# Which quads' C products GpSimdE takes in a Mamba scan, and in which order

## The chip, the cores and the metric

The kernel runs on one core of a Trainium2 chip. The time is the device time of one execution in microseconds (us), the median of some runs. Engines: TensorE (PE in the profile) does matmuls, VectorE (DVE) scans and elementwise work, ScalarE (ACT) activations, GpSimdE (POOL) elementwise work on SBUF only, SyncE (SP) issues the transfers.

## The reference

The input x is (2, 256, 64, 64) in fp32: two batches of 4,096 tokens with 256 channels. Layer 0 is a group norm, a Mamba block with 256 inner channels and a residual. Layer 1 is a layer norm, then a Mamba block forward and one backward (512 inner channels each), residuals, and a mixture of eight small MLPs on all tokens. One Mamba block, cut to what matters here:

```
xs, z = x @ W_in
xs = silu(causal_conv4(xs)); dbc = xs @ W_x
dt = softplus(dbc[:16] @ W_dt + b); B, C = dbc[16:32], dbc[32:48]      # 16 states
h[t, d, s] = exp(dt[t, d] * A[d, s]) * h[t-1, d, s] + dt[t, d] * xs[t, d] * B[t, s]
y[t, d] = sum_s h[t, d, s] * C[t, s] + xs * D
out = (y * silu(z)) @ W_out
```

## The kernel before

The tokens lie along the free axis in chunks of 512, the channels on the 128 partitions. A *job* is one Mamba pass of one batch (layer 0 twice, forward twice, backward twice), a *step* is one chunk of a job: 48 steps, the first 16 narrow (256 inner channels: two blocks of 128, one pair), then 16 forward and 16 backward ones, wide (four blocks, two pairs). For each pair of blocks the 16 states are taken two at a time: a *quad* is two states by two blocks, 128 x 2,048 numbers, n = 0 to 7 counts the quads of a pair, g counts all 640. So a narrow step has one group of eight quads and a wide step two: here called half A (first pair) and half B (second pair).

A quad goes through these functions:

- `load_bc` (line 488) brings the B and C rows of two states from DRAM, broadcast to all partitions (tiles `bc0` and `bc1`, four buffers each).
- `emit_b` (511): GpSimdE makes the product of `xdt` (dt times xc, made at line 509 once per eight quads) and B into the tile `bq` (six buffers). This is the *B product*.
- `emit_decay` (524): ScalarE makes the decays `da` in PSUM, two tiles of two states' halves in turn.
- `emit_scan` (535): VectorE runs four scans of 512 tokens, one per state and block. For even n the result goes into `bq`, for odd n into `da`.
- The *C product*: for even n `emit_times_c_quad` (560) on GpSimdE, in place on `bq`, after `emit_carry` (555), where ScalarE saves the last column as the next chunk's start; for odd n `emit_times_c` (546) on VectorE, with a small copy (549) of the last column.
- `emit_sum` (569): TensorE adds the four parts of `bq` to `y` in PSUM with an identity matrix. The `bq` buffer is free once its sum is done.
- `emit_gate` (585): VectorE multiplies `y` with the gate `sz`; `emit_skip` (578) begins the next `y`, of which there is one buffer.

Beside this the next step's projections are made (`prepare`): in_proj (`xs`, 326) with a copy by ScalarE (351), the convolution as four diagonal matmuls (361), two activations `thx` (370, 371) and VectorE's `xc` (375), x_proj (387), softplus in three activations `sp` (417 to 419) and VectorE's `dt` (423), the gate's `z` and `sz` (444). They share two PSUM buffers (`psp`). `finish` does the output projection (600) and the residual (608) of the step before. `norm` makes the layer norms of the next step. The functions are put into numbered slots for a queue (`Slots`), two slots to a quad, and `prepare` staggers PE, ACT and DVE work by one slot each.

The emission loop at the end runs through the quads and, for both states of each, emits a slot's work for each engine. Every engine's queue is in order. But the framework's scheduler orders the instructions of each queue by priority and by its own estimate of readiness, and assigns tile buffers as they come free in it, so a queue need not stand in the order in which the source emits it.

In the loop GpSimdE's part was, at the first state of each odd n:

```
emit_times_c_quad(g - 1)
want_b(g + 2, g + 3)
want(1, g + 1, g + 2)
want(0, g + 4, g + 5)
```

`want_b` emits B products whose rows are loaded, `want` queues loads (0 for B, 1 for C rows) in one list that `flush` empties from its head. The last stage, the MLPs, comes after all scans.

Of the kernel before, what the change touches and what calls it, by code (L numbers as in the profile page):

```python
# [32 lines left out]
ALU = mybir.AluOpType  # L33
# [7 lines left out]
NS = 16  # L41
DTR = 16
QN = NS // 2
E = 8
V_CW, V_CB, V_DB, V_D, V_A = 0, 4, 5, 6, 7
NV = V_A + NS
# [37 lines left out]
def hybrid_kernel(ctx: ExitStack, tc: tile.TileContext, a: dict, out: bass.AP):  # L84
    nc = tc.nc
# [46 lines left out]
    with ExitStack() as st:  # L132
# [98 lines left out]
        steps = [(job, c) for job in jobs for c in range(NCH)]  # L231
        cks = [{} for _ in steps]
        tags = [f"{n}_{c}" for n in range(len(jobs)) for c in range(NCH)]

        def norm(i, s0, sl):

            (job, c), ck, tag = steps[i], cks[i], tags[i]
            s = job.cols(c)
            b = job.batch

            def alloc():
                ck["nx"] = wk.tile([P, KC, T], F32, tag="nx", name=f"nx_{tag}", bufs=2)

            if job.flip:
                def load():
                    alloc()
                    nc.sync.dma_start(ck["nx"], n2_dram[b][:, NCH - 1 - c, :, :])
                sl.put(s0, "sp", load)
                return

            def load_x():
                alloc()
                ck["x"] = wk.tile([P, KC, T], F32, tag="x", name=f"x_{tag}")
                src = t_dram[b] if job.layer else a["x"][b].rearrange("(k p) l -> p k l", p=P)
                nc.sync.dma_start(ck["x"], src[:, :, s])

            sl.put(max(s0 - 4, 0), "sp", load_x)
            if job.layer == 0:
                def scale():
                    for k in range(KC):  # L260
                        nc.scalar.activation(
                            ck["nx"][:, k, :], ck["x"][:, k, :], AF.Identity,
                            bias=job.gb[:, k : k + 1], scale=job.gs[:, k : k + 1],
                        )
                sl.put(s0, "act", scale)
                return

            def mean():  # L270
                ck["ps"] = psp.tile([P, T], F32, tag="ps", name=f"mean_{tag}")
                for k in range(KC):
                    nc.tensor.matmul(
                        ck["ps"], mean_w, ck["x"][:, k, :], start=(k == 0), stop=(k == KC - 1)
                    )

            def centre():
                ck["cen"] = wk.tile([P, KC, T], F32, tag="cen", name=f"cen_{tag}")
                nc.vector.tensor_tensor(ck["cen"], ck["x"], over_channels(ck["ps"]), ALU.subtract)

            def square():
                ck["n1"] = wk.tile([P, KC, T], F32, tag="n1", name=f"n1_{tag}")
                nc.scalar.activation(ck["n1"], ck["cen"], AF.Square)

            def variance():
                ck["var"] = psp.tile([P, T], F32, tag="ps", name=f"var_{tag}")
                for k in range(KC):
                    nc.tensor.matmul(
                        ck["var"], mean_w, ck["n1"][:, k, :], start=(k == 0), stop=(k == KC - 1)
                    )  # L290

            def roots():
                ck["r1"] = psp.tile([P, T], F32, tag="ps", name=f"r1_{tag}")
                rsqrt(ck["r1"], ck["var"], eps5)
                rsqrt(ck["var"], ck["var"], eps10, scale=1.0 + 1e-5)

            def divide():
                nc.vector.tensor_tensor(ck["n1"], ck["cen"], over_channels(ck["r1"]), ALU.mult)
                nc.vector.tensor_tensor(ck["cen"], ck["cen"], over_channels(ck["var"]), ALU.mult)

            def add():
                nc.gpsimd.tensor_tensor(ck["x"], ck["x"], ck["n1"], ALU.add)

            def affine():
                for k in range(KC):
                    nc.scalar.activation(
                        ck["nx"][:, k, :], ck["cen"][:, k, :], AF.Identity,
                        bias=lngb[:, 1, k : k + 1], scale=lngb[:, 0, k : k + 1],
                    )

            def store():
                nc.sync.dma_start(n2_dram[b][:, c, :, :], ck["nx"])
                nc.sync.dma_start(t_dram[b][:, :, s], ck["x"])

            for d, queue, fn in (
                (0, "pe", mean), (1, "dve", centre), (1, "act", square), (2, "pe", variance),
                (3, "act", roots), (4, "dve", divide), (4, "pool", add), (5, "act", affine),
                (6, "sp", store),
            ):
                sl.put(s0 + d, queue, fn)  # L320

# [15 lines left out]
        def prepare(i, s0, sl, rate=1):  # L337
# [115 lines left out]
            if c == 0:  # L453
                if "in" not in w:
                    load_weights(job, tag, sl)
                    s0 = max(s0, 4)
# [12 lines left out]
            s0 += nj // rate  # L469
            if i + 1 < len(steps):  # L470
                norm(i + 1, s0, sl)
                s0 += 5 if steps[i + 1][0].layer and not steps[i + 1][0].flip else 1
            for j in range(nj):
                put(s0 + j, gate(j))
            return s0 + nj + 2
# [4 lines left out]
        ]  # L480
        nq = len(quads)
        bq, bt, ct, da, y = {}, {}, {}, {}, {}
        loads, wanted = [], []

        def load_bc(g, h, store):
            i, _, n = quads[g]
            t = bcp.tile([P, 2, T], F32, tag=f"bc{h}", name=f"bc{h}_{g}")
            nc.sync.dma_start(t, cks[i]["bc"][h, 2 * n : 2 * n + 2, :].partition_broadcast(P))
            store[g] = t

        def want(h, *gs):
            loads.extend((h, g) for g in gs if g < nq)

        def flush():
            while loads and "bc" in cks[quads[loads[0][1]][0]]:
                h, g = loads.pop(0)
                load_bc(g, h, ct if h else bt)

        def want_b(*gs):
            wanted.extend(g for g in gs if g < nq)  # L500
# [25 lines left out]
                    scale=steps[i][0].w["a"][:, 2 * jp + j, 2 * n + s : 2 * n + s + 1],  # L526
                )

        def emit_scan(g, s):
            i, jp, n = quads[g]  # L530
            job, c = steps[i]
            d = da[g, s]
            for j in range(2):
                b = bq[g][:, s, j, :]
                nc.vector.tensor_tensor_scan(  # L535
                    d[:, j, :] if n % 2 else b, d[:, j, :], b,
                    job.h[:, 2 * n + s, 2 * jp + j : 2 * jp + j + 1] if c else 0.0,
                    ALU.mult, ALU.add,
                )

        def emit_times_c(g, s):

# [16 lines left out]
        def emit_times_c_quad(g):  # L559
            nc.gpsimd.tensor_tensor(  # L560
                bq[g], bq[g],
                ct[g].rearrange("p s (o t) -> p s o t", o=1).to_broadcast([P, 2, 2, T]), ALU.mult,
            )

        def emit_sum(g, ss):
            i, jp, n = quads[g]
            for s in ss:
                for j in range(2):
                    nc.tensor.matmul(  # L569
                        y[i, jp][:, j, :], ident, bq[g][:, s, j, :], start=False,  # L570
                        stop=(n == QN - 2 and s == 1),
                    )

        def emit_skip(i, jp):
# [52 lines left out]
        sl = Slots()  # L627
# [4 lines left out]
        sl.drain(end + 8)  # L632
        want(0, 0, 1, 2)
        want(1, 0, 1)
        want(0, 3, 4)
        flush()
        want_b(0, 1, 2)
        emit_decay(0, 0)
# [3 lines left out]
        for i, (job, c) in enumerate(steps):  # L642
# [3 lines left out]
            if i:  # L646
                finish(i - 1, 3 if wide else 5, sl)
            if i + 1 < len(steps):
                prepare(i + 1, 5 if wide else 0, sl, 1 if wide or steps[i + 1][0].nj == 2 else 2)
            if i < 4:  # L650
                def chunk_stats(k, c=c):
                    v = {}
# [23 lines left out]
            for q in range(np_ * QN):  # L676
                g = g0 + q
                _, jp, n = quads[g]
                for s in range(2):
# [5 lines left out]
                    if first == 2 and last is not None:  # L685
                        emit_gate(*last)
                        last = None
                    sl.run(slot, "dve")

                    if first == 3:  # L690
                        emit_skip(i, jp)
                    sl.run(slot, "pe")
                    if s == 0:
                        if n % 2 == 0:
                            if g >= 1:
                                emit_sum(g - 1, (1,))
                            if g >= 2:
                                emit_sum(g - 2, (0, 1))
                                bq.pop(g - 2)
                                bq.pop(g - 1)  # L700
                                ct.pop(g - 2)
                                ct.pop(g - 1)
                    elif n % 2:
                        emit_sum(g, (0,))
                    if first == 0 and g:
                        pi, pjp, _ = quads[g - 1]
                        last = (pi, pjp)

                    if s == 0 and n % 2:
                        emit_carry(g - 1)  # L710
                    if s == 0:
                        emit_decay(g, 1)
# [1 line left out]
                        emit_decay(g + 1, 0)  # L714
                    sl.run(slot, "act")

                    if s == 0 and n % 2:
                        emit_times_c_quad(g - 1)
                        want_b(g + 2, g + 3)
                        want(1, g + 1, g + 2)  # L720
                        want(0, g + 4, g + 5)
                        flush()
                    sl.run(slot, "pool")

                    emit_scan(g, s)
                    if n % 2:
                        emit_times_c(g, s)
            if sl.at:
                sl.drain(64)
                flush()  # L730
                want_b()
                emit_decay(g + 1, 0)
        g = nq - 1
        emit_sum(g, (1,))
        emit_sum(g - 1, (0, 1))
        i = len(steps) - 1
        emit_gate(i, steps[i][0].nj // 2 - 1)
        sl = Slots()
# [211 lines left out]
```

## Time and profile before

| what | value |
|---|---|
| median of 3 runs (lowest, highest) | 7373.88 us (7371.5, 7379.04) |
| the profiled execution, its span | 7371.24 us, 7369.5 us |
| scans of all quads | from 57 us to 5,601 us |
| MLP stage | from 5,620 us to the end |
| busy TensorE, VectorE, ScalarE, GpSimdE | 83%, 63%, 48%, 62% |
| mean granted TensorE clock | 0.909 |

A share of busy time is taken over the whole span, with the MLP stage in it, where GpSimdE has nothing to do. A group row gives: line, engine, operation, output and inputs with their shapes, count, then busy us and mean ns of one, then the idle time of the engine just before these instructions and what ended most of it. A row of waits gives: who waited, for whom, us in total, times, longest. A row of busy time by stretch gives: the stretch in us from the span's start, its length, then for PE, its weight loads, DVE, ACT and POOL the busy us and count, then the TensorE clock, the DMA share and GB/s. A timeline row gives start, length, engine, line, operation, tiles and count, and in brackets the idle time before it.

### The profile page before, as it was taken

Reading aid. Unit: us, or ns where it says so; the run is one execution under the profiler, and the core shown is the slowest. Engines: PE = TensorE matmul, PEld = TensorE weight load, DVE = VectorE, ACT = ScalarE, POOL = GpSimd, SP = SyncE. Lnnn points to the kernel's source line nnn. Section 1 sums busy time; section 2 is a strip of 40 time slices with the busy share of each in tenths; the row PEclk is TensorE's granted clock in tenths of the full one; section 3 lists DMA queues with packets and bytes.
Section 4 is the critical chain, followed back from the end, with each engine's and each line's share of the span. In section 5 each row is a group of like instructions: output and inputs, shape, how many; then the busy total and the mean of one; then the engine's idle time right before and its main releaser. Section 6 shows DMA issues by size and latency. Waiting matters only on the chain.

```text
span 7369.5 us, 43337 instructions
## 1 busy us (share of the span) xinstructions
PE 6102.4 (83%) x13160; PEld 2613.7 (35%) x13160; DVE 4677.5 (63%) x4889; ACT 3559.7 (48%) x5295; POOL 4535.2 (62%) x1062
## 2 busy tenths in 40 slices
PE   6888778878787888877777778777776999999999
PEld 2333333333333333333333333333333444444444
DVE  6889877778877877877787777787784111111111
ACT  7887556455445555544544544544542222222222
POOL 6889878878878878877887887887883000000000
PEclk8999989999999999988989889888887999999999
DMA  5444434434433443443343343343332000000000
GB/s 187 147 155 167 157 132 158 143 132 140 144 128 132 146 138 129 146 143 129 129 143 124 132 140 123 126 145 125 128 132 94 8 4 12 12 12 12 12 1 11
DMA packets 254189, 806.30 MB, mean 109 GB/s; under 512 B 26362, under 2 KB 35330, under 8 KB 253954
## 3 DMA queue, kind: packets, MB, share of 16 engines
q1 hardware_dynamic: 253954, 803.53, 32.6%
q8 instruction: 103, 1.69, 0.1%
q14 instruction: 132, 1.08, 0.0%
HBM read 749.95 MB, written 53.48 MB: 109 GB/s over the span
## 4 chain that ended last, share of the span: by engine, by line
POOL 27%; PE 22%; issue 16%; DVE 2%; ACT 1%; DMA 1%; POOLq 0%; SPq 0%; DVEq 0%; ACTq 0%
POOL bq L511 19%; PE hp L835 13%; POOL bq L560 7%; PE ym L869 6%; PE wb L860 1%; POOL xdt L509 1%; PE lg L805 1%; PE var_m L125 1%; DVE bq L535 1%; DVE da L535 1%; PE ym L855 0%; DMA t_dram<-xr 0%; ACT L108 0%; DVE cen_m L118 0%; DMA xr<-t_dram 0%
## 5 line engine op out<-in xcount | busy, mean ns | idle before, releaser
L511 POOL TENSOR_TENSOR bq<-xdt,bc 128x2048 f32<-128x2048 f32 x640 | 2880.7, 4523 | 555.0 <-PE y L569 553.4
L524 ACT ACTIVATE da<-dt,w_a 128x512 f32<-128x512 f32 x2564 | 1751.9, 689 | 1965.6 <-DVE h_state L549 1010.4
L569 PE MATMUL y<-bq,ident 128*128 128x512 f32 x5120 | 2363.6, 608 | 88.1 <-POOL bq L560 51.2
L535 DVE TENSOR_TENSOR_SCAN bq<-da,h_state,bq 128x512 f32<-128x512 f32 x1120 | 1360.0, 1267 | 631.9 <-POOL bq L511 605.2
L560 POOL TENSOR_TENSOR bq<-bq,bc 128x2048 f32<-128x2048 f32 x320 | 1447.6, 4524 | 311.8 <-ACT h_state L555 305.8
L569 PEld LDWEIGHTS y<-bq,ident 128*128 128x128 f32 x5120 | 1002.4, 197 | 1397.3 <-issue 1262.0
L535 DVE TENSOR_TENSOR_SCAN da<-da,h_state,bq 128x512 f32<-128x512 f32 x1120 | 1410.7, 1280 | 61.2 <-ACT da L524 31.4
L839 ACT ACTIVATE h<-hp,of,sc 128x512 f32<-128x512 f32 x512 | 398.4, 778 | 1024.1 <-PE hp L835 1024.1
L361 PE MATMUL conv<-xs,w_conv 128*128 128x512 f32 x1280 | 681.0, 682 | 249.0 <-ACT xs L351 248.1
L546 DVE TENSOR_TENSOR bq<-da,bc 128x1024 f32<-128x1024 f32 x640 | 778.8, 1218 | 12.7
L578 PE MATMUL y<-xc,w_d 128*128 128x512 f32 x320 | 275.0, 1009 | 541.2 <-DVE sz L585 541.2
L866 DVE TENSOR_TENSOR h<-h,wbs 128x1024 f32<-128x1024 f32 x128 | 156.9, 1226 | 874.7 <-ACT h L839 874.7
L361 PEld LDWEIGHTS conv<-xs,w_conv 128*128 128x128 f32 x1280 | 273.8, 219 | 641.5 <-issue 333.8
L835 PE MATMUL hp<-n,W 128*128 128x512 f32 x1024 | 490.4, 633 | 0.0
L835 PE MATMUL hp<-h,W 128*128 128x512 f32 x1024 | 449.9, 592 | 0.0
L869 PE MATMUL ym<-h,Wo 128*128 128x512 f32 x1024 | 449.9, 592 | 0.0
L326 PE MATMUL z<-nx,w_in 128*128 128x512 f32 x640 | 321.6, 635 | 133.4 <-DVE sz L444 76.7
L578 PEld LDWEIGHTS y<-xc,w_d 128*128 128x128 f32 x320 | 88.7, 303 | 680.5 <-DVE sz L585 599.7
L326 PE MATMUL xs<-nx,w_in 128*128 128x512 f32 x640 | 302.5, 604 | 15.0 <-DVE sz L444 5.9
L600 PE MATMUL o<-sz,w_out 128*128 128x512 f32 x640 | 311.9, 624 | 1.1 <-DVE sz L444 0.8
L835 PEld LDWEIGHTS hp<-n,W 128*128 128x128 f32 x1024 | 200.9, 202 | 293.4 <-issue 293.4
L509 POOL TENSOR_TENSOR xdt<-dt,xc 128x1024 f32<-128x1024 f32 x80 | 188.4, 2355 | 187.8 <-DVE dt L423 165.1
(121 smaller groups left out, 4424.2 us busy)
## 6 DMA issues: line engine op xcount, KB each, us to landing
bc<-bcd SPq DMA_DIRECT2D x1280, 512.0 KB, 3.9
t_dram<-xr SPq DMA_DIRECT2D x48, 512.0 KB, 3.6
x<-t_dram SPq DMA_DIRECT2D x32, 512.0 KB, 5.7
xr<-t_dram SPq DMA_DIRECT2D x32, 512.0 KB, 5.2
x<-in_x SPq DMA_DIRECT2D x16, 512.0 KB, 5.1
xr<-in_x SPq DMA_DIRECT2D x16, 512.0 KB, 3.8
t_dram<-x SPq DMA_DIRECT2D x16, 512.0 KB, 3.1
n_dram<-nx SPq DMA_DIRECT2D x16, 512.0 KB, 4.0
```

The costliest lines, as they stand in the source:

```text
L326: nc.tensor.matmul(ps, job.w["in"][:, k, m * P : (m + 1) * P], rhs, start=(k == 0), stop=(k == KC - 1),)
L361: nc.tensor.matmul(v["ps"], w["conv"][:, j, k, :], job.xs[:, j, k : k + T], start=(k == 0), stop=(k == 3),)
L511: nc.gpsimd.tensor_tensor(bq[g], ck["xdt", jp].rearrange("p (o j) t -> p o j t", o=1).to_broadcast([P, 2, 2, T]), bt.pop(g).rearrange("p s ...
L524: nc.scalar.activation(da[g, s][:, j, :], cks[i]["dt", jp][:, j, :], AF.Exp, scale=steps[i][0].w["a"][:, 2 * jp + j, 2 * n + s : 2 * n + s ...
L535: nc.vector.tensor_tensor_scan(d[:, j, :] if n % 2 else b, d[:, j, :], b, job.h[:, 2 * n + s, 2 * jp + j : 2 * jp + j + 1] if c else 0.0, ...
L546: nc.vector.tensor_tensor(bq[g][:, s, :, :], d, ct[g][:, s : s + 1, :].to_broadcast([P, 2, T]), ALU.mult)
L560: nc.gpsimd.tensor_tensor(bq[g], bq[g], ct[g].rearrange("p s (o t) -> p s o t", o=1).to_broadcast([P, 2, 2, T]), ALU.mult,)
L569: nc.tensor.matmul(y[i, jp][:, j, :], ident, bq[g][:, s, j, :], start=False, stop=(n == QN - 2 and s == 1),)
L578: nc.tensor.matmul(y[i, jp][:, j, :], job.w["d"][:, 2 * jp + j, :], cks[i]["xc", jp][:, j, :], start=True, stop=False,)
L835: nc.tensor.matmul(ps, w[:, k, m * P : (m + 1) * P], x[:, k, :], start=(k == 0), stop=(k == KC - 1),)
L839: nc.scalar.activation(h[:, m, :], ps, AF.Relu, bias=of[:, l, e, m : m + 1], scale=sc[:, l, e, m : m + 1],)
L869: nc.tensor.matmul(y[:, b, m, :], we["Wo", e][:, k, m * P : (m + 1) * P], h2[b][:, k, :], start=False, stop=(e == E - 1 and k == KC - 1),)
```

## The change

GpSimdE takes the C products of quads 0, 2, 3 and 5 of each eight in place of 0, 2, 4 and 6. A table `POOL_C` gives for each of these the later quad at whose start its sum is emitted on TensorE (0 at 2, 2 at 4, 3 at 5, 5 at 7). A table `POOL_AT` gives the order in which GpSimdE's products are emitted at the start of a quad ("c0 b4 b5" at quad 1: the C product of quad 0, then the B products of quads 4 and 5), and each B product emits the load of the B rows three quads later. C rows are wanted two quads ahead, one per quad, and the loads of B and C rows have lists of their own. VectorE's slot work (projections) is emitted between the two scans of a state in place of ahead of them. `prepare` begins one slot earlier in wide steps, and the normalisation's activations and later parts are one slot later. The core of the diff:

```diff
+POOL_C = {0: 2, 2: 4, 3: 5, 5: 7}
+POOL_AT = {0: "b3", 1: "c0 b4 b5", 3: "c2 b6", 4: "c3 b7", 6: "c5 b8 b9", 7: "b10"}
...
-                (0, "pe", mean), (1, "dve", centre), (1, "act", square), (2, "pe", variance),
-                (3, "act", roots), (4, "dve", divide), (4, "pool", add), (5, "act", affine),
-                (6, "sp", store),
+                (0, "pe", mean), (1, "dve", centre), (2, "act", square), (3, "pe", variance),
+                (4, "act", roots), (5, "dve", divide), (6, "pool", add), (6, "act", affine),
+                (7, "sp", store),
...
-        def emit_scan(g, s):
+        def emit_scan(g, s, j):
...
+            b = bq[g][:, s, j, :]
+            nc.vector.tensor_tensor_scan(
+                b if n in POOL_C else d[:, j, :], d[:, j, :], b,
...
-                prepare(i + 1, 5 if wide else 0, sl, 1 if wide or steps[i + 1][0].nj == 2 else 2)
+                prepare(i + 1, 4 if wide else 0, sl, 1 if wide or steps[i + 1][0].nj == 2 else 2)
...
-                    sl.run(slot, "dve")
...
+                        if g and (n - 1) % QN not in POOL_C:
+                            emit_sum(g - 1, (1,))
+                        for m, due in POOL_C.items():
+                            if due == n:
+                                emit_sum(g - n + m, (0, 1))
+                    elif n not in POOL_C:
                         emit_sum(g, (0,))
...
-                    if s == 0 and n % 2:
-                        emit_times_c_quad(g - 1)
-                        want_b(g + 2, g + 3)
-                        want(1, g + 1, g + 2)
-                        want(0, g + 4, g + 5)
+                    if s == 0:
+                        for what in POOL_AT.get(n, "").split():
+                            m = g - n + int(what[1:])
+                            if what[0] == "c":
+                                emit_times_c_quad(m)
+                            else:
+                                want(0, m + 3)
+                                flush()
+                                want_b(m)
+                    else:
+                        want(1, g + 2)
                         flush()
                     sl.run(slot, "pool")
 
-                    emit_scan(g, s)
-                    if n % 2:
+                    emit_scan(g, s, 0)
+                    sl.run(slot, "dve")
+                    emit_scan(g, s, 1)
+                    if n not in POOL_C:
                         emit_times_c(g, s)
```

## The prediction

> **What bounds the kernel now.** Read the page's first part and the three groups of the scan loop, then the waits, then the busy time by half step.
>
> ```profile
> PE 6102.4 (83%) x13160; PEld 2613.7 (35%) x13160; DVE 4677.5 (63%) x4889; ACT 3559.7 (48%) x5295; POOL 4535.2 (62%) x1062
> ...
> L511 POOL TENSOR_TENSOR bq<-xdt,bc 128x2048 f32<-128x2048 f32 x640 | 2880.7, 4523 | 555.0 <-PE y L569 553.4
> ...
> L535 DVE TENSOR_TENSOR_SCAN bq<-da,h_state,bq 128x512 f32<-128x512 f32 x1120 | 1360.0, 1267 | 631.9 <-POOL bq L511 605.2
> L560 POOL TENSOR_TENSOR bq<-bq,bc 128x2048 f32<-128x2048 f32 x320 | 1447.6, 4524 | 311.8 <-ACT h_state L555 305.8
> ```
>
> No engine is full. All GpSimdE work lies in the 5,540 us of the scans: 80 groups of eight quads, each 12 products of 4.52 us and one xdt of 2.36, so 56.6 us per group. The waits show a ring: VectorE waits for GpSimdE's B products, these wait for TensorE's sums to free a buffer, TensorE waits for ScalarE's copies:
>
> ```profile
> DVE bq L535 <- POOL bq L511: 694.3, 243, 7.5
> ...
> POOL bq L511 <- PE y L569: 553.4, 85, 10.1
> POOL bq L560 <- ACT h_state L555: 305.8, 201, 7.7
> ...
> PEld conv L361 <- ACT xs L351: 303.9, 68, 6.5
> ```
>
> Busy time by half step: two halves (A, then B) of a backward step, then of a forward step.
>
> ```profile
> 4087.80:4154.90 67.10, 52.16 (x109) 22.22 (x108) 51.85 (x53) 25.84 (x42) 53.92 (x13) 0.85 0.48 157
> 4154.90:4227.80 72.90, 57.46 (x126) 24.46 (x125) 56.75 (x60) 41.09 (x64) 58.63 (x15) 0.93 0.33 109
> 2681.10:2749.40 68.30, 57.01 (x117) 24.09 (x116) 53.98 (x57) 27.45 (x46) 56.20 (x15) 0.88 0.51 169
> 2749.40:2823.90 74.50, 58.41 (x127) 24.57 (x126) 57.76 (x60) 46.71 (x71) 58.54 (x15) 0.93 0.33 107
> ```
>
> Columns: length, then busy us of PE, its loads, DVE, ACT, POOL. A backward step takes 140.0 us with VectorE busy 108.6: it stands 31.4. So the time is set by who stands ahead of whom in the queues. GpSimdE's timeline shows it:
>
> ```profile
> 4127.71 9.00 POOL L511 TENSOR_TENSOR bq<-xdt,bc 128x2048 f32<-128x2048 f32 x2 [1.81 <-PE y L569]
> 4137.45 4.52 POOL L560 TENSOR_TENSOR bq<-bq,bc 128x2048 f32<-128x2048 f32 x1 [0.73 <-ACT h_state L555]
> 4150.39 8.98 POOL L511 TENSOR_TENSOR bq<-xdt,bc 128x2048 f32<-128x2048 f32 x2 [8.42 <-PE y L569]
> 4160.10 4.52 POOL L560 TENSOR_TENSOR bq<-bq,bc 128x2048 f32<-128x2048 f32 x1 [0.73 <-ACT h_state L555]
> ```
>
> One C product, two B products, one C product: the two Bs wait for a late sum, and no B product is ahead.
>
> **What the skill says.** The Trainium skill, "GPSIMD Engine Reference", Performance versus the Vector engine: a two-input fp32 operation on 2048 elements takes 4497 ns on GpSimdE; here 4523 and 4524. "TensorE: Matmul & The Clock Gate", The HAM clock gate: after an idle window of about 3.4 us the array runs at half rate until busy for as long. Agrees: eight convolution instructions took 6.62 us after 4.03 us of idleness, 3.60 without.
>
> ```profile
> 4138.53 6.62 PE L361 MATMUL conv<-xs,w_conv 128*128 128x512 f32 x8 [4.03 <-ACT xs L351]
> ```
>
> "ScalarE: Activation LUTs", What ACT_TABLE_LOAD costs: 1283 ns and a drain of about 1380. The trace has the 1283; the next activation starts 0.02 us after it, so I charge 1.28.
>
> **The change part by part.** Work on GpSimdE, TensorE and VectorE keeps its count and size: four C products per group, 12 GpSimdE products, the same scans. So nothing is gained or lost in busy time there; only order counts. The built program (its queues can be read without running it) does not hold the order in the table POOL_AT: the scheduler moves products by its own estimate. In the built program of before, a wide group reads c0 b2 b3 c2 b4 b5 c4 b6 b7 c6 b0' b1' (b is a quad's B product, c its C product, ' the next group), as the timeline above has it. After, in backward steps:
>
> - A: c0 b2 b3 b4 c2 b5 c3 c5 b6 b7 b8
> - B: c8 b9 b10 c10 b11 b12 c11 b13 x b14 c13 b15 x b0' b1'
>
> In forward steps A is c0 b3 b4 c2 b5 c3 c5 b6 b7 b8, and B has x c13 b14 b15 x, add, b0' b1' b2'. So c5 stands ahead of b6, c8 of b9, c10 of b11, c11 of b13: the next quad's B product waits behind a C product that can't begin before the scan just done. Behind that B product stand VectorE's scan, then ScalarE's decays (they need the scan's PSUM tile back) with the projection's copies, then TensorE's convolutions and sums.
>
> I work this as a timetable with the durations of before's trace: a product 4.52; a quad whose C is on GpSimdE 4.8 (four scans, 4.81 in VectorE's timeline); a quad with C on VectorE 7.4 (4137.00 to 4144.47); from scan to C product 0.4 (ScalarE's carry copy); two matmuls of a sum 1.72. t is 0 at the first scan of A in a backward step.
>
> A. c0 5.2 to 9.7, b2 to 14.3, b3 18.8, b4 23.3, c2 27.8, b5 32.3, c3 36.8. VectorE: q1 to 12.2, q2 14.3 to 19.1, q3 to 23.9, q4 with the gate and one residual add to 33.2, q5 with the other to 38.7. c5 (carry at 38.3) to 42.9, b6 47.4, b7 51.9: q6 starts at 47.5, **8.8 idle**. TensorE gets the gate at 26.3, does skip, output projection, sums 5 and 0, and the first convolution by 48.9, the third xs by 50.6; its copy on ScalarE stands behind the decays of q7, which wait for q6 (54.9), so it ends at 58.5. The second convolution runs cold, 58.6 to 65.2, then sum 2 to 68. b8 needs that buffer: 68 to 72.6. q7 ended at 63.5: **9 idle**. A is 72.6 (now 67.1).
>
> B. q8 to 77.4, xc to 78.1, c8 77.8 to 82.3, b9 86.8 (**8.8 idle**), b10 91.3. q9 86.9 to 94.3, q10 with xc to 100. c10 100.4 to 104.9, b11 109.4 (**9.5 idle**), b12 113.9, q11 to 114.3, c11 119.2, b13 123.7, x 126.9. Softplus: table loads are 8 per backward step in place of 4 (416 to 531 in all; 416 is what the page's table-load rows sum to), as the softplus chains no longer run in pairs. q12 ends at 125.8, q13's decays and dt follow ScalarE to 137 (**5 lost**), its carry at 138.4. b14 to 134.7, q14 to 147.1 with two sz; c13 143, b15 147.5, x 149.9, q15 to 156.4; b0' needs sum 10, which stands behind a z projection that waits for sz: 152.5 to 157. Period **157.0**, now 140.0: **+17**.
>
> Forward: b0' b1' b2' are ahead of c0, and the normalisation's add ahead of b0'. q6 begins at 48.8, B's start shifts to 72.9; c13 (ready 138.9) is ahead of b14, so q14 begins at 148 in place of 138.3. With three normalisation operations (3.6) it ends at 157.6, q15 and the next start follow at **164.5**; now 140.7 and 142.7 in turn, so **+22.8**.
>
> Narrow steps (16, 1,074 us, 67.1 each): as built, b0 to b5 precede c0 in most. GpSimdE alone would allow 56.6, but sum 0 and the output projection behind it wait for the late c0, and VectorE's residual add for these. I work out 61 to 66 for ten of them, up to 72 for the last six, where c5 again precedes b6: about -60 to +60 in all, taken as 0.
>
> VectorE's projection work between two scans: the waits it can hide are xc for thx, 209.3 us (96 waits), and dt for sp, 55.1, so at most 264; at worst it frees a PSUM buffer one scan (1.2 us) later, some 10 times a step, 48 steps, 576. In the built queue xc stands behind the product before it, and in A the wait for b8 covers it: 0 beyond the timetable. The split load lists and the normalisation one slot later: the same 1,280 loads, landing in 3.9 us (median), needed over 9 us later by the timetable; if that cover goes, 3.9 for each late load. Nothing else moves on SP's queue. The last stage (1,750 us after 5,620) is untouched.
>
> Sum: 15 x 17 + 16 x 22.8 = 255 + 365 = 620. On the profiled execution's own 7371.2 (span 7369.5): 7991. The median shown is 7373.9, 2.7 above; I say **7990**.
>
> **Rivals.**
> - *Half of it* (chance 0.28). The timetable follows every wait at its worst; TensorE's cold runs and the doubled table loads may be hidden while VectorE stands for GpSimdE anyway. Without cold runs and ScalarE's delays a backward step is some 148, a forward one 154: 15 x 8 + 16 x 12 = 312, giving 7680.
> - *Faster* (0.08). TensorE's lateness goes: a longer chain through GpSimdE gives it time, b8 no longer waits for sum 2, and the chain of scans and products alone decides: A 62.2, B 74, 136.2 in place of 140, or 31 x 3.8 = 118, giving about 7255. Against: the second convolution's copy stands behind q7's decays whatever TensorE does. It decides once sum 2 is there before b7 ends (51.9).
> - *No change* (0.03). The lost and the won idle time cancel, 7374; also if the order on the chip were not the built one, but before's timeline has its built order.
> - The forecast (0.61): 7990, own range 7800 to 8160.
>
> **The numbers.** About 0.2% (15 us) is what a measurement of this kernel can tell from no change. Faster 0.08, same 0.03, slower 0.89. The range takes most of the halved case and the narrow steps' bounds: 7620 to 8160.
>
> **What would show it.** GpSimdE's share falls to some 57%. VectorE's wait for B products rises from 694 to some 1,500 us, in waits of about 9 us. C product to B product to scan, with VectorE idle from the scan before, four times per wide step. Wide steps of 150 to 165 us. Table loads 531. It would be wrong if B halves stay under 75 us, or if the B products in the trace run ahead of the C products.

## The result, and the profile after

The changed kernel takes 7935.66 us (median of 4 runs, 7934.25 to 7937.73); the kernel before, on the same chip, 7373.19 (7371.5 to 7379.04). The ratio is 1.0762, 95% interval 1.0743 to 1.078: 562 us slower. The profiled execution's span is 7932.4 us. Where the 562 us lie, read from the starts of the quads' first scans in both traces:

| part of the run | before | after | difference |
|---|---|---|---|
| narrow steps (16) | 1073.8 | 1100.2 | +26.4 |
| forward wide steps (16) | 2257.4 | 2559.1 | +301.7 |
| backward wide steps (to the last half) | 2156.3 | 2390.5 | +234.2 |
| last half, to the start of its last quad | 44.7 | 44.7 | 0 |

The page of after: the busy times, GpSimdE's two groups, the two groups of scans.

```profile
PE 6202.5 (78%) x13160; PEld 2658.0 (34%) x13160; DVE 4669.0 (59%) x4889; ACT 3693.2 (47%) x5406; POOL 4532.1 (57%) x1062
...
L515 POOL TENSOR_TENSOR bq<-xdt,bc 128x2048 f32<-128x2048 f32 x640 | 2878.3, 4517 | 555.8 <-PE y L572 553.2
...
L563 POOL TENSOR_TENSOR bq<-bq,bc 128x2048 f32<-128x2048 f32 x320 | 1446.3, 4521 | 861.0 <-ACT h_state L558 848.1
L538 DVE TENSOR_TENSOR_SCAN da<-da,h_state,bq 128x512 f32<-128x512 f32 x1120 | 1398.3, 1279 | 603.5 <-POOL bq L515 553.5
L538 DVE TENSOR_TENSOR_SCAN bq<-da,h_state,bq 128x512 f32<-128x512 f32 x1120 | 1357.6, 1265 | 558.6 <-POOL bq L515 447.0
```

GpSimdE and VectorE do what they did before, to within 0.2% (4532 and 4669 us busy, from 4535 and 4678). What grew is idle time: 861 us ahead of the C products (312 before) and 1162 us ahead of the scans in these two groups (631.9 and 61.2 before, 693). The waits give the pairs:

```profile
POOL bq L563 <- ACT h_state L558: 848.1, 190, 11.0
...
DVE da L538 <- POOL bq L515: 625.2, 104, 9.4
...
POOL bq L515 <- PE y L572: 553.2, 66, 15.5
DVE bq L538 <- POOL bq L515: 532.1, 104, 9.7
```

VectorE's wait for B products is 625.2 + 532.1 = 1157 us in place of 703 (694.3 and 8.7). GpSimdE stands for the copy of a last column (`h_state`, ScalarE) about as often as before, 190 times for 201, but for 848 us in place of 306. For transfers it stands 14 us in all, so the split load lists are not where the time went. The wait for TensorE's sums is the same in total, but its longest is 15.5 us for 10.1.

Busy time by half step (columns as before): A and B of a backward step, then B and the next A of forward steps.

```profile
4497.40:4567.28 69.88, 51.94 (x113) 22.46 (x112) 51.89 (x54) 27.07 (x44) 53.49 (x12) 0.88 0.41 143
4567.28:4651.69 84.41, 58.14 (x121) 24.68 (x120) 56.21 (x60) 44.85 (x66) 58.92 (x15) 0.84 0.28 101
2509.10:2599.08 89.98, 62.81 (x126) 26.49 (x125) 55.69 (x60) 49.05 (x71) 64.54 (x16) 0.85 0.31 106
2599.08:2668.63 69.55, 55.01 (x116) 23.41 (x115) 54.04 (x57) 29.44 (x49) 50.15 (x12) 0.88 0.42 143
```

The loss is mostly in the second halves: 84.4 for 72.9 backward, 90.0 for 74.5 forward, with VectorE no busier than before (56.2 for 56.8, 55.7 for 57.8). GpSimdE's timeline from the end of A through B shows how; L563 is a C product, L515 a B product:

```profile
4534.91 4.53 POOL L563 TENSOR_TENSOR bq<-bq,bc 128x2048 f32<-128x2048 f32 x1 [1.25 <-ACT h_state L558]
4539.38 8.99 POOL L515 TENSOR_TENSOR bq<-xdt,bc 128x2048 f32<-128x2048 f32 x2
4562.48 4.51 POOL L515 TENSOR_TENSOR bq<-xdt,bc 128x2048 f32<-128x2048 f32 x1 [14.11 <-PE y L572]
4572.19 4.52 POOL L563 TENSOR_TENSOR bq<-bq,bc 128x2048 f32<-128x2048 f32 x1 [5.21 <-ACT h_state L558]
4576.68 8.96 POOL L515 TENSOR_TENSOR bq<-xdt,bc 128x2048 f32<-128x2048 f32 x2
4594.59 4.52 POOL L563 TENSOR_TENSOR bq<-bq,bc 128x2048 f32<-128x2048 f32 x1 [8.95 <-ACT h_state L558]
4599.06 8.97 POOL L515 TENSOR_TENSOR bq<-xdt,bc 128x2048 f32<-128x2048 f32 x2
```

These are c5, b6 b7, b8, c8, b9 b10, c10, b11 b12. Each C product is followed by the B product that VectorE needs next, and VectorE's timeline (scans only) has a wait at each of those:

```profile
4543.94 4.82 DVE L538 TENSOR_TENSOR_SCAN da<-da,h_state,bq 128x512 f32<-128x512 f32 x4 [8.81 <-POOL bq L515]
...
4567.02 4.81 DVE L538 TENSOR_TENSOR_SCAN bq<-da,h_state,bq 128x512 f32<-128x512 f32 x4 [4.05 <-POOL bq L515]
...
4581.21 4.82 DVE L538 TENSOR_TENSOR_SCAN da<-da,h_state,bq 128x512 f32<-128x512 f32 x4 [5.64 <-POOL bq L515]
...
4603.61 4.81 DVE L538 TENSOR_TENSOR_SCAN bq<-da,h_state,bq 128x512 f32<-128x512 f32 x4 [9.38 <-POOL bq L515]
```

At 4572 GpSimdE stands 5.21 us for ScalarE's copy of q8, which can't be taken before q8 is scanned; then it makes c8 (4.52), which no scan needs, and only then b9 (4.5): VectorE idles 5.64 us. The same at q6 and q11. The 14.11 us ahead of b8 are another thing. TensorE's timeline:

```profile
4546.62 1.02 PE L572 MATMUL y<-bq,ident 128*128 128x512 f32 x2
4554.60 5.21 PE L365 MATMUL conv<-xs,w_conv 128*128 128x512 f32 x8 [6.96 <-ACT xs L355]
4559.65 2.74 PE L572 MATMUL y<-bq,ident 128*128 128x512 f32 x6
```

The sum of q2 begins at 4546.62 with two of its eight instructions; behind them in TensorE's queue stands the second convolution, which waits 6.96 us for ScalarE's copy, and the other six follow it. They end at 4562.39, and b8, which by the prediction's reading takes q2's buffer, starts at 4562.48.

### The profile page after: what moved, and what is told of

Read it like the earlier page. It is cut to its first block, busy times and chain, and to the rows that moved or that the text cites. A ratio compares the mean times of both kernels' runs of the same rounds, so it can differ in the third digit from the quotient of the medians.

```text
span 7932.4 us, 43494 instructions
## 1 busy us (share of the span) xinstructions
PE 6202.5 (78%) x13160; PEld 2658.0 (34%) x13160; DVE 4669.0 (59%) x4889; ACT 3693.2 (47%) x5406; POOL 4532.1 (57%) x1062
## 4 chain that ended last, share of the span: by engine, by line
issue 31%; POOL 31%; PE 23%; DVE 8%; ACT 3%; DMA 2%; SPq 0%; POOLq 0%; DVEq 0%; ACTq 0%
POOL bq L515 23%; PE hp L841 12%; POOL bq L563 7%; PE ym L875 6%; DVE da L538 3%; DVE bq L538 2%; POOL xdt L513 2%; DVE bq L549 1%; PE y L572 1%; ACT da L528 1%; PE wb L866 1%; PE lg L811 1%; PE var_m L129 1%; DMA bc<-bcd 1%; DMA t_dram<-xr 1%
## 5 line engine op out<-in xcount | busy, mean ns | idle before, releaser
L515 POOL TENSOR_TENSOR bq<-xdt,bc 128x2048 f32<-128x2048 f32 x640 | 2878.3, 4517 | 555.8 <-PE y L572 553.2
L563 POOL TENSOR_TENSOR bq<-bq,bc 128x2048 f32<-128x2048 f32 x320 | 1446.3, 4521 | 861.0 <-ACT h_state L558 848.1
L365 PE MATMUL conv<-xs,w_conv 128*128 128x512 f32 x1280 | 654.4, 659 | 276.9 <-ACT xs L355 275.9
L330 PE MATMUL z<-nx,w_in 128*128 128x512 f32 x640 | 369.2, 718 | 230.0 <-DVE sz L448 112.6
L391 PE MATMUL dbc<-xc,w_x 128*128 128x512 f32 x320 | 192.8, 731 | 362.1 <-DVE xc L379 308.1
```

The costliest lines, as they stand in the source:

```text
L330: nc.tensor.matmul(ps, job.w["in"][:, k, m * P : (m + 1) * P], rhs, start=(k == 0), stop=(k == KC - 1),)
L365: nc.tensor.matmul(v["ps"], w["conv"][:, j, k, :], job.xs[:, j, k : k + T], start=(k == 0), stop=(k == 3),)
L515: nc.gpsimd.tensor_tensor(bq[g], ck["xdt", jp].rearrange("p (o j) t -> p o j t", o=1).to_broadcast([P, 2, 2, T]), bt.pop(g).rearrange("p s ...
L563: nc.gpsimd.tensor_tensor(bq[g], bq[g], ct[g].rearrange("p s (o t) -> p s o t", o=1).to_broadcast([P, 2, 2, T]), ALU.mult,)
```

## The experiments

All are timed in three rounds beside the kernel before (7372.6 to 7380.9 us in their groups). Gains below 0.2% are read as none, and a difference between experiments of different groups is good to some 8 us.

**1. GpSimdE held in the order of emission.** The framework has an edge of order between two instructions of one engine (`tc.issue_after`), without a semaphore. Chaining all products in the order in which the source emits them keeps the scheduler from moving them: a group then reads c0 b4 b5 c2 b6 c3 b7 c5 x b0' b1' b2' b3'.

```diff
+    def queued(name, fn):
+        with ExitStack() as es:
+            if name in prev:
+                es.enter_context(tc.issue_after(prev[name]))
+            fn()
+        prev[name] = nc.cur_bb.bb.instructions[-1]
...
-            nc.gpsimd.tensor_tensor(
+            queued("pool", lambda: nc.gpsimd.tensor_tensor(
```

> The changed kernel with GpSimdE's queue held in the order in which the source emits it (c0 b4 b5 c2 b6 c3 b7 c5 x b0' b1' b2' b3'), nothing else edited; the built queues of TensorE, VectorE and ScalarE stay nearly as they were, with 531 table loads. Theory (the order on GpSimdE's queue, C product ahead of the next quad's B product, costs the 562 us): VectorE's waits for B products fall from 1157 us to under 500, time 7350 to 7600. Rivals (VectorE's projection work between the scans, or ScalarE's 115 more table loads, or the choice of quads, costs it): all three are still there, so 7850 to 7950.

Measured 7658.23 us (7656.41 to 7660.47), ratio 1.0388 (1.0372 to 1.0403): 277 us of the 562 go when GpSimdE is held. Less than expected: VectorE's waits for B products fall from 1157 to 955 us (487.8 and 467.4), not under 500. The wait for ScalarE's copies is gone (40.4 us), and another has taken its place:

```profile
POOL bq L525 <- PE y L582: 1044.8, 142, 14.1
```

Both sides of the longest of these in a second half, GpSimdE first, then TensorE:

```profile
4391.35 4.50 POOL L525 TENSOR_TENSOR bq<-xdt,bc 128x2048 f32<-128x2048 f32 x1 [11.84 <-PE y L582]
```

```profile
4378.85 2.74 PE L401 MATMUL dbc<-xc,w_x 128*128 128x512 f32 x6
4385.77 2.08 PE L401 MATMUL dbc<-xc,w_x 128*128 128x512 f32 x2 [4.18 <-DVE xc L389]
4387.64 4.93 PE L582 MATMUL y<-bq,ident 128*128 128x512 f32 x7
```

Half the sum of q6 stands behind the x projection (dbc), and that waits for VectorE's last xc. VectorE has its scans first.

**2. The kernel before, held in the same way.** The same edit on the kernel before; a group reads c0 b3 b4 c2 b5 b6 c4 b7 c6 x b0' b1' b2'.

> The kernel before with GpSimdE's queue held in its emission order (c0 b3 b4 c2 b5 b6 c4 b7 c6 x b0' b1' b2'), so that each B product stands one to two quads earlier. Theory: part of before's own 694 us of VectorE waiting for B products goes, time 7150 to 7350; TensorE's late sums then decide. If the order on GpSimdE's queue is no bound, 7360 to 7390.

Measured 7390.82 us (7388.07 to 7391.63), ratio 1.0025 (1.0016 to 1.0034): not the gain expected, a little slower. GpSimdE stands 463.6 us for TensorE's sums and now 247.5 for arriving B and C rows. So the order of emission is no gain with the old quads; in the changed kernel it was one against the order that the scheduler had built there.

**3. VectorE's place, and the normalisation.** The kernel before, with VectorE's slot work between the two scans and the normalisation, with the gates behind it, a slot later. The second half of the edit touches only the work for forward steps.

```diff
-                s0 += 5 if steps[i + 1][0].layer and not steps[i + 1][0].flip else 1
+                s0 += 6 if steps[i + 1][0].layer and not steps[i + 1][0].flip else 1
...
-                    sl.run(slot, "dve")
...
-                    emit_scan(g, s)
+                    emit_scan(g, s, 0)
+                    sl.run(slot, "dve")
+                    emit_scan(g, s, 1)
```

> The kernel before with only the change to VectorE's placement: projection work between the two scans of a state, and the normalisation's later parts one slot later, which this needs; quads 0, 2, 4, 6 as before. The built GpSimdE order is before's but for some halves with one B product further ahead; 416 table loads. Theory (order on GpSimdE): 7330 to 7400. Rival (VectorE's placement frees PSUM and the softplus late): 7650 to 7930.

Measured 7283.73 us (7280.11 to 7287.4), ratio 0.9881 (0.9865 to 0.9898): 89 us faster than the kernel before, more than expected. The forward steps are 100.6 us shorter (2156.8 for 2257.4): most first halves take 59 us in place of 66 to 68, and in these b2 is now built ahead of c0. The backward steps, in which VectorE's place is the only thing moved, take 2156.3 us in both kernels. So the gain is not shown to be VectorE's place: it may as well be the later normalisation, and no run moves that alone.

**4. VectorE's place taken back.** The changed kernel with that work ahead of both scans again, the normalisation left where the change has it.

```diff
                     emit_scan(g, s, 0)
-                    sl.run(slot, "dve")
                     emit_scan(g, s, 1)
...
+                    sl.run(slot, "dve")
```

> The changed kernel with VectorE's projection work ahead of both scans again; quads 0, 2, 3, 5 and the tables kept. The built GpSimdE order keeps c0 b1, c2 b3, c5 b6; 528 table loads. Theory (order on GpSimdE): 7850 to 7980. Rival (VectorE's placement): 7370 to 7650.

Measured 7931.83 us (7927.71 to 7933.19), ratio 1.0758 (1.0742 to 1.0774): the same as after. In the changed kernel VectorE's place is worth nothing.

**5. One pair exchanged.** In the changed kernel, one edge: c0 of a group is put behind b1 of it.

```diff
+            made[g] = nc.cur_bb.bb.instructions[-1]      # in emit_b
...
+            if quads[g][2] == 0 and g + 1 in made:
+                es.enter_context(tc.issue_after(made[g + 1]))
```

> The kernel after with one pair exchanged in GpSimdE's queue: where a second half begins with c8 b9 b10 c10, an edge of order puts b9 first (b9 c8 b10 c10); the rest of the built queue is as it was, and so are the 531 table loads. In the trace of after c8 stands 5.2 us for ScalarE's copy of q8's last column, and VectorE then stands 5.6 us for b9. Theory (the order of GpSimdE's queue is what costs): b9 is made in the time in which GpSimdE stood for c8, some 4 to 5 us less for each of 31 second halves, 7780 us (7740 to 7850). Rival (another wait takes its place, the late sums of TensorE or VectorE's own chain): 7900 to 7940. In the trace the wait for b9 goes and second halves take 79 to 81 us instead of 85.

Measured 7801.62 us (7798.04 to 7806.03), ratio 1.0572 (1.0556 to 1.0587): 134 us less, 4.3 for each of 31 second halves, as worked out. Those of backward steps take mostly 80.5 to 81.4 us in place of 84.4 to 85.1, those of forward steps 85.3 in place of 89.7 on average, and the quad q8 8.6 in place of 14.2. Nothing else in GpSimdE's queue moved.

**6 and 7. ScalarE's table loads.** The held changed kernel, and the kernel before, with softplus's last function replaced by one that takes as long (0.72 and 0.71 us) and leaves out 315 and 203 table loads. Both then compute another `dt`; only the time is read.

```diff
-                    nc.scalar.activation(v["th"], v["th"], AF.Ln, bias=one_col)
+                    nc.scalar.activation(v["th"], v["th"], AF.Identity, bias=one_col)
```

> The kernel after with GpSimdE held in the order of emission (7658 us), in which softplus's third function (Ln) is replaced by Identity with the same bias: its output is another, each instruction stays in its place and has the same shape, and ScalarE's table loads fall from 531 to 216. Theory (the 115 loads that the change added, and ScalarE's softplus chains that hold up the decays of quads 12 to 15, make up much of the 285 us that are left over the kernel before): 7450 to 7560. Rival (the late sums on TensorE that keep GpSimdE from its buffers decide, and ScalarE's waits beside them are covered): 7610 to 7660. If the table loads are a cost common to both kernels, the kernel before gains as much when its Ln is replaced.

> The kernel before with Ln replaced by Identity in softplus in the same way (its output is another): 416 table loads become 213. It is the measure for the same edit on the changed kernel. Theory (the added loads are what the change pays): the kernel before gains little, 7330 to 7372, and the held changed kernel much more. Rival (loads cost both alike, about 203 x 1.28 us = 260 us of ScalarE's time of which some is on the path): 7150 to 7300.

The held changed kernel takes 7470.81 us (7467.19 to 7474.34), 187 less than with Ln; the kernel before 7299.08 (7297.07 to 7300.33), 81 less than its 7379.93. So both gain, as the rival had it for the kernel before, and the changed one by 106 more. That these 106 us are what the 115 added loads cost is not shown. By the traces, in which the two gains differ by 112 us, 66.6 lie in the forward steps (126.4 - 59.8), 31.9 in the narrow ones (33.8 - 1.9) and 11.7 in the backward steps (25.3 - 13.6). But of the 115 loads the change added 54 in the forward steps, 9 in the narrow ones and 52 in the backward ones: nine loads of 1.28 us can't be 31.9 us. And in experiment 7 the scheduler also built b2 ahead of c0 in most forward first halves, as in experiment 3.

**8. The four quads.** Experiment 3 held in the order of emission: the quads 0, 2, 4, 6 beside experiment 1's 0, 2, 3, 5, with the same place for VectorE's work (the load lists and the slot at which `prepare` begins differ as well).

> The kernel before (C products of quads 0, 2, 4, 6) with the changed kernel's place for VectorE's work and norm, and with GpSimdE held in the order of emission: against the held changed kernel (7658 us) it differs in the four quads, and in how far ahead their B products and sums stand. Theory (the four quads and the buffers that their late sums hold are the rest of the loss): 7300 to 7390. Rival (the place of VectorE's work, or the held order itself, is what costs): 7550 to 7660.

Measured 7406.32 us (7404.64 to 7407.91), ratio 1.0035 (1.0021 to 1.0049), 252 less than experiment 1, 16 above the theory's range. Whether it is the quads or where their sums stand isn't told apart by this run. The next one moves the sums.

**9. TensorE's sums ahead of the projections.** Experiment 1, with one line moved: in each slot the projections' matmuls are emitted behind the sums.

```diff
-                    sl.run(slot, "pe")
                     if s == 0:
                         if g and (n - 1) % QN not in POOL_C:
...
                     elif n not in POOL_C:
                         emit_sum(g, (0,))
+                    sl.run(slot, "pe")
```

> The kernel after with GpSimdE held in the order of emission (7658 us), in which TensorE's sums are emitted ahead of the projections of their slot instead of behind them: in the built queue the sums of q6 and q5 now stand ahead of the x projection (dbc), which waits for VectorE's last xc; 519 table loads instead of 531. In the trace of the held kernel GpSimdE stood 1044.8 us for TensorE's sums, up to 11.8 us in one second half for the sum of q6 that lies behind dbc. Theory (these sums, which release the B buffers, are what is left of the loss after the order and the table loads): a gain of 4 to 7 us for each of 31 wide steps, 7440 to 7550. Rival (VectorE or ScalarE is then late by as much): 7610 to 7660.

Measured 7248.43 us (7247.77 to 7249.32), ratio 0.982 (0.9804 to 0.9837): 410 us less than experiment 1, nearly twice the most that was expected, and 1.8% faster than the kernel before. GpSimdE makes its B and C products in the order of experiment 1; the table loads are 519 in place of 531. The page's groups and two half steps:

```profile
L525 POOL TENSOR_TENSOR bq<-xdt,bc 128x2048 f32<-128x2048 f32 x640 | 2883.0, 4521 | 754.8 <-PE y L582 602.2
...
L573 POOL TENSOR_TENSOR bq<-bq,bc 128x2048 f32<-128x2048 f32 x320 | 1448.1, 4525 | 33.9 <-ACT h_state L568 33.9
...
L375 PE MATMUL conv<-xs,w_conv 128*128 128x512 f32 x1280 | 612.8, 628 | 52.4 <-ACT xs L365 49.6
```

```profile
3999.04:4061.54 62.50, 48.87 (x103) 20.91 (x102) 51.60 (x53) 25.27 (x42) 55.77 (x13) 0.86 0.46 160
4061.54:4135.57 74.03, 61.52 (x132) 25.88 (x131) 56.87 (x61) 45.75 (x69) 56.52 (x14) 0.91 0.33 115
```

The wait for sums is 602 us in place of 1045, and the idle time ahead of the convolutions is 52 us, where experiment 1 had 158 and after 276.9: with its sums early, GpSimdE is early, VectorE's scans are, and so ScalarE's copies. That the ring so lets go as a whole would explain why the gain is larger than the one wait that was read; it is read from these waits, not shown by a run of its own.

**10. The same on experiment 3.** Quads 0, 2, 4, 6, the scheduler's order on GpSimdE, sums ahead of the projections.

> The kernel before with VectorE's projection work between two scans and norm a slot later (7284 us), with TensorE's sums emitted ahead of the projections of their slot; 465 table loads instead of 416. If late sums matter in the kernel before as they do in the changed one: 7200 to 7260. If GpSimdE's order (a C product ahead of the next B product) decides there, and the sums don't: 7270 to 7320, the 49 added loads at 0.9 us each among it.

Measured 7452.53 us (7449.76 to 7454.54), ratio 1.0096 (1.0081 to 1.0112): 169 us slower than experiment 3, which neither reading expected. The 49 added loads, 63 us if each cost its full 1.28, can't be all of it. In a second half, GpSimdE's pair b12 b13 now waits 6.2 us for a sum, where in experiment 3 it waited for nothing. TensorE's queue tells what delays that sum; the first two lines are of this run, the third is of experiment 3:

```profile
3675.91 2.07 PE L387 MATMUL dbc<-xc,w_x 128*128 128x512 f32 x2 [3.79 <-DVE xc L375]
3677.77 7.10 PE L568 MATMUL y<-bq,ident 128*128 128x512 f32 x12
...
3524.16 3.60 PE L387 MATMUL dbc<-xc,w_x 128*128 128x512 f32 x8
```

With twelve sum instructions ahead of it, the half's last convolution ends some 24 us after the half's start in place of 18. VectorE then has the scans of q10 and most of q11 ahead of the last xc, the x projection (dbc) stands for that xc, and the next sums stand behind the x projection. So sums first made other sums late. This order is read in one half, but the wait is not of one half: TensorE stands 118.7 us in 33 places ahead of the x projection for xc (there are 32 wide steps), where in experiment 3 it stood 2.1 us. In the changed kernel the same move did the opposite, 133.2 us in experiment 1 and 6.5 in experiment 9. In first halves and in forward steps the scheduler changed GpSimdE's order too, so the 169 us need not all be of this kind.

**11. B products further ahead in the kernel before.** Experiment 3 with c0 of each group behind b2 of it (the edge of experiment 5, with g + 2).

> The kernel before with VectorE's projection work between two scans and norm a slot later (7284 us), with one edge of order in each half: the C product of quad 0 is held behind the B product of quad 2. The built queue of a half is then c0 b3 c2 b4 in second halves and c0 b3 b4 c2 in first halves, instead of c0 b2 b3 c2 and, in backward first halves, c0 b2 b3 b4; the 416 table loads stay. Theory (a B product that VectorE needs next must not stand behind a C product that waits for ScalarE's copy): 3 to 7 us less in each of 15 backward first halves and 31 second halves, 7030 to 7180. Rival (B buffers and sums bound GpSimdE as soon as it is no longer behind): 7250 to 7300.

Measured 7381.93 us (7374.73 to 7384.35), ratio 0.9999 (0.9991 to 1.0008): 98 us slower than experiment 3, a miss. Backward second halves take 78.2 us in place of 72.8. GpSimdE's timeline there:

```profile
4150.58 4.51 POOL L512 TENSOR_TENSOR bq<-xdt,bc 128x2048 f32<-128x2048 f32 x1 [15.34 <-PE y L573]
```

This is b10: put ahead of c8, it stands 15.34 us for a buffer whose sum isn't made, and c8 stands behind it. Here the C product's operand was there first; in experiment 5 it was the B product's.

**12. Experiment 9's move without the hold.** The changed kernel with the same line moved, GpSimdE left to the scheduler.

> The kernel after (7936 us) with TensorE's sums emitted ahead of the projections of their slot, and GpSimdE's queue left to the scheduler: the fourth corner beside after, the held order alone (7658 us) and both edits (7248 us). GpSimdE's built queue differs from after's in first halves alone, where b6 now stands ahead of c5; second halves still begin c8 b9 b10 c10. In the trace of after GpSimdE stood 553.2 us for TensorE's sums (14.1 us in the one first half read) and 848.1 us for ScalarE's column copies. Theory (each order costs by itself, and the two add): some 400 us less, 7500 to 7600. Rival (the C products that stand for ScalarE's copies hold GpSimdE for as long as the sums did, so that the sums alone gain little): 7780 to 7940.

Measured 7651.56 us (7648.03 to 7654.81), ratio 1.0369 (1.0352 to 1.0386), between the two expectations. With it the four corners are complete:

| | GpSimdE as the scheduler orders it | GpSimdE held |
|---|---|---|
| sums behind the projections | 7935.7 (after) | 7658.2 |
| sums ahead | 7651.6 | 7248.4 |

Holding GpSimdE takes away 277 us, the moved line 284, both 687, 126 more than their sum. But in the left column the moved line is not the sums alone. In the trace of experiment 12 the scheduler has put b6 ahead of c5 in first halves and b14 ahead of c13 in forward second halves; after has them the other way round (the expectation knew of the first halves alone). Of the 289 us by which the traces' scan stages differ, only 24 lie in the backward second halves, where GpSimdE's order is the same as in after (83.1 us in place of 84.4 to 85.1 in most). In first halves, now mostly 67 us (backward) and 64 (forward) in place of 70 to 72, VectorE's wait ahead of q6 has gone from 8.8 to between 2 and 4 us and from 9.4 to under 1. And b8 of a backward step still stands for its sum, nearly as long as the 14.11 us in after:

```profile
3874.32 4.51 POOL L515 TENSOR_TENSOR bq<-xdt,bc 128x2048 f32<-128x2048 f32 x1 [12.39 <-PE y L572]
```

So what the sums' place alone is worth under the scheduler's order stays open. The right column compares it with GpSimdE's order unchanged: 410 us. Apart from 12 table loads, the four do the same work.

## Why the prediction was right

**The forecast: 7990, range 7620 to 8160, slower 0.89. Measured 7935.7.** The cause that it named, the built order in which a C product stands ahead of the next B product, is shown by experiments 1 and 5, and the first halves of experiment 12 agree. Its second link, the late sum of q2 ahead of b8, stands in the timeline above; no run takes away that one wait (experiment 12 leaves 12.39 us of it). That sums behind the projections cost time at all is shown by experiment 9, for the held kernel.

**Half A, 72.6.** Measured 69.9 to 71.3 in most backward steps. The idle time at q6 came as worked out (8.8; measured 8.81). The chain copy, cold convolution, sum 2, b8 was placed at 58.6 to 72.6 from the start of A; in the trace it runs from 57.2 to 69.6. It began 1.4 us sooner, and the cold convolution was taken too large, 6.62 from a row of before, 5.21 here: after 6.96 idle us its first four instructions took 0.77 to 1.22 us and the rest the usual 0.59. The 9 us ahead of q8 were 4.05, as A ended sooner while q7 took longer.

**Half B, 84.4 backward.** Measured 84.4 and 85.1 in the two read: q9's wait was 5.6 instead of 8.8, q11's 9.38 for 9.5. The smaller wait at q9 isn't a gain, since q8 with VectorE's xc was as long as forecast (14.2 for 14.3).

**The sums.** Backward +17 a step gave 255; measured 234.2 over 15.5 steps, 15.1 each. Forward +22.8 gave 365; measured 301.7, 18.9 each, as a step takes 159.9 on average in place of 164.5: B is 89.7 for 91.6, A 70.2 for 72.9. These two terms were too large by 84 us together. Narrow steps were taken as 0 within 60 either way; measured +26.4, all of it in the last six (431.9 to 458.3). They take 76.4 each, more than the 72 that the prediction allowed, which is what they took before. In the trace c5 stands ahead of b6 in three of the six, not in all, and these three make 18.5 of the 26.4 us.

**VectorE's work between two scans, taken as 0.** Right for the changed kernel (experiment 4). The reason given, that the wait for B products covers it, is not shown: in the backward steps of the kernel before the same edit changes nothing either (experiment 3). The 89 us that experiment 3 gains lie in the forward steps, where the normalisation was moved as well.

**Table loads.** 531 as forecast. The "5 lost" per backward step came in size, as far as the length of the two quads tells: q12 and q13 of backward second halves take 12.6 and 10.8 us, 23.4 for the 22.7 worked out. That the added loads are its cause is not shown; between experiments 6 and 7 the gains of all backward steps differ by 11.7 us, under 1 a step.

**What would show it.** GpSimdE's share 57% as said. VectorE's wait for B products rose to 1157, not 1500: waits of 9 us came at two places in a wide step rather than four, with 4 to 6 us at the others, and VectorE's projection work and other waits lie in between.

**The rivals.** *Half of it* said that TensorE's cold runs and ScalarE's delays would be hidden behind GpSimdE's. In the trace they were not: b8 waits 14.11 us behind the cold convolution and VectorE then 4.05 for b8, and q12 and q13 are as long as worked out. No run takes these two away alone. *No change* fell. *Faster* did not come either; it needed the sum of q2 in time, and put A at 62.2, B at 74 and the time at 7255. With GpSimdE held and the sums moved, experiment 9 has A at 62.5, B at 74.0 and 7248. That the figures agree so closely is in part luck: the rival keeps the scheduler's order of products, experiment 9 has the source's; B products still stand 602 us for sums in it; and 25.3 of the 122.9 us between its trace and that of before lie in narrow steps, which the rival left out. Nor is it what the source as it stands is worth: that has the sums behind the projections, and held to it GpSimdE gives 7658 (experiment 1).

Left open: whether quads 0, 2, 3, 5 are better than 0, 2, 4, 6 as such. The best of each measured, experiment 9 and experiment 3, are 7248 and 7284; the sums ahead with the old quads and GpSimdE held were not run. Nor was the earlier start of `prepare` or the later normalisation taken back alone.

## What to carry to other kernels

When a change sets an order in the source, read the built queue before you believe in it: here the scheduler put C products ahead of the B products that the next scan needed, and the source itself has matmuls that wait for a late operand ahead of the sums that free buffers. In a ring of engines, look in each in-order queue for the instruction that waits longest and at what stands behind it without needing it; with GpSimdE held, moving one line so that buffer-freeing work goes first was worth 410 us. Compare two edits only when the queues that you didn't mean to touch are the same: a line moved on TensorE also changed GpSimdE's built order. A place in the order is good or bad only against the operand that comes last: moves of the same kind, B products first or sums first, cost 98 and 169 us in the kernel with the old quads.

## What was not expected of the hardware

A table load on ScalarE is 1.28 us in every trace, but leaving loads out saved less than that on the clock: 187 us for 315 fewer in the held kernel (0.59 each), and 81 for 203 fewer in the kernel before (0.40 each, with GpSimdE's order changed in forward first halves). And the mean granted TensorE clock is lower in the kernel that waits more, 0.880 in after for 0.908 in experiment 9, with the same 13,160 matmuls busy 6202 and 6115 us. These two numbers don't show which is the cause.
